# The first modulation rows as full-width products of the repeated silu(c), read in place by the first norm

## The chip, the cores and the metric

The kernel runs on one core of a Trainium2 chip. Its time is the device time of one execution in microseconds. The core has TensorE (PE, with its weight loads shown apart as PEld), VectorE (DVE), ScalarE (ACT), GpSimd (POOL) and the sync engine (SP), whose queue issues nearly all DMAs. PE writes to PSUM; the other engines read PSUM or SBUF.

## The reference

The kernel computes one transformer block with adaptive layer norm: attention without a softmax, then a mixture of eight experts. Two sequences of 1024 tokens, width 512, all float32. What matters here is how the first norm is modulated:

```python
mod = (_silu(L0_c) @ L0_wmod).reshape(L0_c.shape[0], 6, 1, -1)   # c: (2, 512), wmod: (512, 3072)
sa, ca, ga, sb, cb, gb = (mod[:, i] for i in range(6))
h = _layernorm(x, axis=-1) * (1 + ca) + sa
x = x + ga * attention(h)      # attention starts with a second layernorm, then K, V = Xn @ W_in + b_in
h = _layernorm(x, axis=-1) * (1 + cb) + sb
x = x + gb * moe(h)
```

Each of the six rows is one row of 512 values for each sequence. The first norm needs ca and sa of the first sequence on every one of the 128 partitions, since a partition holds a token.

## The kernel before

The 2048 tokens are 16 tiles of 128; tiles 0 to 7 are the first sequence, 8 to 15 the second, and four tiles share one x buffer and one buffer xnT of normed, transposed activations. For each tile t the kernel does: **norm1_in** (mean and variance of x: two DVE instructions, a square root on ACT, a reciprocal on DVE), **norm1_mid** (h = (x - mean) * (1 + ca)), **norm1_out** (h = h * rs + sa, then the second norm: statistics of h, sd, rs, off, and hn on ACT), **turn1** (four transposes of hn on PE into PSUM, four evictions by ACT into xnT), **kv_half** for K and for V (four products of 128x512 each, accumulated, evicted by DVE with the bias b_kv) and **kv_back** (squares, products and an accumulation on ACT, DVE and POOL). This loop over the tiles of the first sequence is the kernel's first stage; later come the projection, the second norm, the routing, the expert blocks and the shared expert.

Ahead of the loop stands the **opening**. PE first runs turn_over, products whose result nobody reads. The rows come from line 232, mod_parts: silu(c), padded to 32 columns in sc_pad, is the stationary operand, and the four 128-row pieces of the weights wm_ca (or wm_sa) are multiplied in four column strips of the array, each strip giving a partial sum for its piece k. ACT copies these partial sums to SBUF (parts). A second product, line 284, spread_product, has as its stationary operand one column of pick, repeated 128 times: it adds up the four partial sums of a sequence and puts the sum on all partitions at once. ACT copies that to SBUF, adding 1 for ca (spread_copy). The second sequence's rows are spread in the same place and copied a little later, though no tile before 8 reads them.

Buffers named by a home are shared: home 1 holds wm_sa first and xnT_0 afterwards, home 0 holds wm_ca and later wm_gb.

What orders the work: each engine runs its instructions in a fixed order. That order is made when the kernel is built, from the order in the program and a model of when inputs are ready, so it can differ from the program's. `tc.issue_after(ins)` puts the instructions in its block that run on ins's engine behind ins. DMAs go to SP's queue in the order of the load lines 152 to 204: c, wm_ca, the first x tile, wm_sa, cols, the other three x tiles of the group, the two halves of w_kv, b_kv, the rope table cs, and then the rest.

Of the kernel before, what the change touches and what calls it, by code (L numbers as in the profile page):

```python
# [18 lines left out]
P = 128  # L19
# [5 lines left out]
def kernel(  # L25
# [129 lines left out]
    def load_mod(m, home):  # L155
        t = act_tile(home, f"wmod{m}")
        nc.sync.dma_start(t, wm[:, :, m * D : (m + 1) * D])
        return t
# [3 lines left out]
    def load_x(g):  # L162
        t = xpool.tile([P, 4, D], FP, tag="x", name=f"x{g}")
        xs[g] = t
        for j0, j1 in ((0, 1), (1, 4)) if g == 0 else ((0, 4),):
            nc.sync.dma_start(t[:, j0:j1], xf[g][:, j0:j1])
            yield
# [40 lines left out]
    nc.vector.memset(ones_row, 1.0)  # L208
# [8 lines left out]
    nc.scalar.activation(sig_c, csb, AF.Sigmoid)  # L217
# [12 lines left out]
    copied = []  # L230

    def mod_parts(m, w, t):
        ps = mm_ps(f"mod_{m}")
        for k in range(KC):
            nc.tensor.matmul(
                ps[k * CT : (k + 1) * CT, :],
                sc_pad[:, k, :],
                w[:, k, :],
                start=True,
                stop=True,  # L240
                tile_position=(0, k * CT),
            )
        copied.append(nc.scalar.copy(t, ps))
# [35 lines left out]
    def own_parts(m, w):  # L279
        t = kvp.tile([P, D + 2 * R2], FP, tag="pr", name=f"parts_{m}")[:, 0:D]  # L280
        mod_parts(m, w, t)
        return t

    def spread_product(t, b, tag):
        ps = mm_ps(f"{tag}_{b}")
        nc.tensor.matmul(
            ps, pick[:, b : b + 1].to_broadcast([P, P]), t, start=True, stop=True
        )
# [7 lines left out]
    def spread_now(t, b, plus, tag):  # L296
        return spread_copy(spread_product(t, b, tag), b, plus, tag)
# [18 lines left out]
    aggregated = {}  # L316
# [9 lines left out]
    def normalize(dst, src, name):  # L326
        mv = small.tile([P, 2], FP, tag="mv", name=f"mv_{name}")
        rs = small.tile([P, 1], FP, tag="rs", name=f"rs_{name}")
        moments(mv, rs, src, name)
        off = small.tile([P, 1], FP, tag="off", name=f"off_{name}")  # L330
        nc.vector.tensor_scalar(off, mv[:, 0:1], -1.0, rs, ALU.mult, ALU.mult)
        nc.scalar.activation(dst, src, AF.Identity, bias=off, scale=rs)
# [15 lines left out]
    hn_of, turned1 = {}, {}  # L348
# [17 lines left out]
    def norm1_out(t):  # L366
        h, b = h_of.pop(t), t // NJ
        nc.vector.scalar_tensor_tensor(h, h, rs1[:, t : t + 1], sa[b], ALU.mult, ALU.add)
        hn_of[t] = ln.tile([P, D], FP, tag="hn", name=f"hn_{t}")
        normalize(hn_of[t], h, f"b{t}")  # L370
# [30 lines left out]
    fronts = {}  # L401
    waiting = []

    def kv_half(t, i):
# [4 lines left out]
        for k in range(KC):  # L409
            nc.tensor.matmul(  # L410
# [8 lines left out]
        )  # L419
        if i == 0 and waiting:  # L420

            with tc.issue_after(ins.ins):
                waiting.pop()()
# [636 lines left out]
    def second_rows():  # L1060


        return (
            spread_product(parts_ca, 1, "ca1"),
            spread_product(parts_sa, 1, "sa"),
        )

# [8 lines left out]
    def other_sums():  # L1076
# [8 lines left out]
        0: [],  # L1085
# [20 lines left out]
    norm1_out(0)  # L1106
    norm1_mid(1)
    turn1(0)
    with tc.issue_after(turned1[0].ins):
        ca1[1] = spread_copy(rows_1[0], 1, ones_t[:, 0:1], "ca1")  # L1110
        sa[1] = spread_copy(rows_1[1], 1, zero_t, "sa")
    norm1_out(1)
    acc = start_acc(0)
    for t in range(NJ):
        if t == 0:
            norm1_mid(2)
            norm1_out(2)

            nc.vector.scalar_tensor_tensor(
                cs[:, :, 0, :], cs[:, :, 1, :], -2.0, cs[:, :, 0, :], ALU.mult, ALU.mult  # L1120
            )
            nc.vector.scalar_tensor_tensor(
                cs[:, :, 1, :], cs[:, :, 1, :], -2.0, cs[:, :, 1, :], ALU.mult, ALU.mult
            )
            nc.vector.tensor_scalar(cs[:, :, 1, :], cs[:, :, 1, :], 1.0, None, ALU.add)
# [3 lines left out]
        turn1(t + 1)  # L1129
        for step in side[t]:  # L1130
            step()
        kv_half(t, 1)
# [575 lines left out]
```

## Time and profile before

| | us |
|---|---|
| median of 3 runs | 769.61 (768.76 to 770.23) |
| the profiled execution | 772.12 |
| its span, first to last instruction | 770.3 |
| PE busy | 751.9 |
| first stage opens: first kv product of tile 0 starts | 18.94 |

A line of a timeline reads: start in us, length in us (of a merged group: first start to last end), engine, line of the kernel, operation, output<-inputs, shape, count, and in brackets the idle time of that engine just before it with what ended it. A line of the waits or groups gives idle time by what released it. The granted clock of PE over the whole run was 0.994.

### The profile page before, as it was taken

Reading aid. Unit: us, or ns where it says so; the run is one execution under the profiler, and the core shown is the slowest. Engines: PE = TensorE matmul, PEld = TensorE weight load, DVE = VectorE, ACT = ScalarE, POOL = GpSimd, SP = SyncE. Lnnn points to the kernel's source line nnn. Section 1 sums busy time; section 2 is a strip of 40 time slices with the busy share of each in tenths; the row PEclk is TensorE's granted clock in tenths of the full one; section 3 lists DMA queues with packets and bytes.
Section 4 is the critical chain, followed back from the end, with each engine's and each line's share of the span. In section 5 each row is a group of like instructions: output and inputs, shape, how many; then the busy total and the mean of one; then the engine's idle time right before and its main releaser. Section 6 shows DMA issues by size and latency. Waiting matters only on the chain. (4 is left out here: it accounts for less than half of the span.)

```text
span 770.3 us, 8477 instructions
## 1 busy us (share of the span) xinstructions
PE 751.9 (98%) x2527; PEld 415.8 (54%) x2527; DVE 428.7 (56%) x979; ACT 232.5 (30%) x495; POOL 214.9 (28%) x241
## 2 busy tenths in 40 slices
PE   7999999999999999999999999999999998999997
PEld 2444444444444444684565656656566554888542
DVE  3888956898736888982222123222221121499964
ACT  4664523557643153110122122221221212122310
POOL 1234524863632687562100000000000000234530
PEclk9999999999999999999999999999999999999999
DMA  8950001212335711367999999999999884624551
GB/s 322 383 170 16 14 0 69 109 57 67 137 96 195 269 68 42 123 260 252 337 352 347 348 344 334 343 339 325 330 338 331 292 287 161 193 83 136 166 163 55
DMA packets 96369, 158.91 MB, mean 206 GB/s; under 512 B 8089, under 2 KB 51097, under 8 KB 96321
## 3 DMA queue, kind: packets, MB, share of 16 engines
q1 hardware_dynamic: 89984, 138.41, 53.6%
q0 software_dynamic: 5760, 18.88, 7.4%
q10 hardware_dynamic: 576, 1.05, 0.4%
q8 instruction: 22, 0.36, 0.2%
q14 instruction: 27, 0.21, 0.1%
HBM read 128.15 MB, written 30.16 MB: 206 GB/s over the span
## 5 line engine op out<-in xcount | busy, mean ns | idle before, releaser
L1360 POOL DMA_INDIRECT y<-ybuf,yrows x32 | 37.0, 1156 | 336.0 <-SPq L1586 288.4
L410 PE MATMUL kv<-w_kv,xnT 128*128 128x512 f32 x256 | 115.2, 596 | 0.5 <-ACT xnT L393 0.5
L1486 PE MATMUL by<-wd_r,gtT 128*128 128x512 f32 (+1 forms) x210 | 96.1, 593 | 0.8 <-DVEq L1578 0.8
L1458 PE MATMUL bg<-wg_r,hbT 128*128 128x352 f32 x280 | 88.9, 460 | 0.9 <-ACT y L1490 0.9
L1458 PE MATMUL bu<-wu_r,hbT 128*128 128x352 f32 x280 | 88.5, 459 | 0.0
L410 PEld LDWEIGHTS kv<-w_kv,xnT 128*128 128x128 f32 x256 | 46.9, 190 | 57.2 <-issue 48.1
L1458 PEld LDWEIGHTS bu<-wu_r,hbT 128*128 128x128 f32 x280 | 53.2, 190 | 29.6
L1473 DVE COPY gtT<-gtr 128x256 f32<-128x256 f32 x35 | 14.9, 425 | 97.0 <-PE gtr L1470 97.0
L1458 PEld LDWEIGHTS bg<-wg_r,hbT 128*128 128x128 f32 x280 | 50.4, 190 | 23.5 <-ACT y L1490 1.3
L571 PE MATMUL o<-wp,xnT 128*128 128x512 f32 x128 | 57.3, 593 | 0.0
L1337 DVE TENSOR_TENSOR sg_b<-sg_b,bg 128x352 f32<-128x352 f32 x35 | 18.3, 521 | 68.8 <-ACT sg_b L1336 68.8
L1486 PEld LDWEIGHTS by<-wd_r,gtT 128*128 128x128 f32 (+1 forms) x210 | 37.2, 191 | 34.5 <-issue 33.5
L1450 ACT COPY hbT<-tr_b 128x512 f32<-128x512 f32 x36 | 21.1, 586 | 101.1 <-PE tr_b L337 101.1
L1338 DVE TENSOR_TENSOR gt<-sg_b,bu 128x352 f32<-128x352 f32 x35 | 18.3, 521 | 47.2 <-PE bu L1458 47.2
L1490 ACT COPY y<-by 128x512 f32<-128x512 f32 x35 | 20.5, 586 | 70.7 <-PE by L1486 48.9
L571 PEld LDWEIGHTS o<-wp,xnT 128*128 128x128 f32 x128 | 23.8, 190 | 28.6 <-issue 27.0
L1336 ACT ACTIVATE sg_b<-bg 128x352 f32<-128x352 f32 x35 | 16.2, 464 | 76.1 <-PE bg L1458 76.1
L440 POOL TENSOR_TENSOR cross<-kv 128x128 f32<-128x128 f32 x16 | 12.6, 790 | 75.4 <-DVE kv L417 45.2
L530 PE MATMUL wp<-aw,wqT 128*128 128x512 f32 x64 | 30.0, 625 | 0.7 <-DVE aw L511 0.7
L433 ACT ACTIVATE sq<-kv 128x512 f32<-128x512 f32 x32 | 20.2, 630 | 27.2 <-DVE kv L417 25.6
L610 POOL TENSOR_TENSOR hr<-hr,cb 128x512 f32<-128x512 f32 x16 | 22.3, 1393 | 21.3 <-issue 7.2
L393 ACT ACTIVATE xnT<-tr_a,colsb 128x128 f32<-128x128 f32 x64 | 24.4, 455 | 11.0 <-PE tr_a L337 10.9
(319 smaller groups left out, 1264.7 us busy)
## 6 DMA issues: line engine op xcount, KB each, us to landing
wg_r<-in_w_gate_dram SPq DMA_DIRECT2D x35, 704.0 KB
wu_r<-in_w_up_dram SPq DMA_DIRECT2D x35, 704.0 KB
wd_r<-in_w_down_dram SPq DMA_DIRECT2D x35, 512.0 KB
hb<-hbuf SPq DMA_DIRECT2D x36, 256.0 KB
ybuf<-y SPq DMA_DIRECT2D x31, 256.0 KB
wd_r<-in_w_down_dram SPq DMA_DIRECT2D x35, 192.0 KB
wmod<-in_wmod_dram SPq DMA_DIRECT2D x6, 1024.0 KB
x<-in_x_dram SPq DMA_DIRECT2D x3, 1024.0 KB
```

Of the source, the lines that this page charges most:

```text
L393: turned1[t] = nc.scalar.activation(xnT[g][:, f, j * P : (j + 1) * P], ps[:, f * P : (f + 1) * P], AF.Identity, bias=colsb[:, 1, f : f + 1 ...
L410: nc.tensor.matmul(ps, xnT[g][:, k, j * P : (j + 1) * P], w_kv[:, i, k, :], start=(k == 0), stop=(k == KC - 1),)
L433: nc.scalar.activation(sq, kv[:, i, :], AF.Square, accum_out=ss[:, i : i + 1])
L530: nc.tensor.matmul(ps, wqT[:, k, f * P : (f + 1) * P], aw[:, k, :], start=(k == 0), stop=(k == KC - 1),)
L571: nc.tensor.matmul(ps, xnT[g][:, k, j * P : (j + 1) * P], wp[:, k, :], start=(k == 0), stop=(k == KC - 1),)
L610: nc.gpsimd.tensor_mul(h, h, cb1[b])
L1337: nc.vector.tensor_mul(sg[:m, :n], sg[:m, :n], pg[:m, :n])
L1360: nc.gpsimd.indirect_dma_start(out=y, out_offset=None, in_=ybuf, in_offset=bass.IndirectOffsetOnAxis(ap=yrows[:, t, s : s + 1], axis=0), b ...
L1450: nc.scalar.copy(hbT.rearrange("p k q -> p (k q)"), ps)
L1458: nc.tensor.matmul(ps[:, :H], hbT[:, k, :], wt[:, k, :], start=(k == 0), stop=(k == KC - 1))
L1486: nc.tensor.matmul(ps, gtT[:m, c, :], w[2][:m, c, :], start=(c == 0), stop=(c == NH - 1))
L1490: nc.scalar.copy(y, ps)
```

## The change

The rows are made in another way, and the opening is put in another order.

1. row_product takes the place of mod_parts and spread_product for ca and sa. One column of silu(c) is repeated 128 times as the stationary operand, and the four pieces of the weights are accumulated over the full array, so that the sum stands on all partitions at once. For ca a product of ones with a row of 1/128 is accumulated first, which adds the 1. The results stay in the PSUM pool sh (three buffers), and norm1_mid(0) and norm1_out(0) read them there; ACT copies them for the later tiles. The second sequence's row products come ahead of turn1(0), and their copies behind turn1(1).
2. wm_ca is loaded in two pieces, wm_sa in four, the first x tile ahead of both; the x tiles 2 and 3 behind the first half of w_kv; b_kv in two halves.
3. A square root of a constant behind the sigmoid loads ACT's table for it early.
4. norm1_in(1), norm1_out(1), norm1_in(2), norm1_mid(2) and norm1_out(2) get their places by issue_after. In the first pass of the loop both kv halves come ahead of turn1(1), and the three operations on cs come behind the second kv eviction.
5. turn_over has four products ahead of the rows instead of three, and none behind them.

mod_parts stays for the other four rows.

```diff
-    def load_mod(m, home):
+    def load_mod(m, home, pieces=1):
         t = act_tile(home, f"wmod{m}")
-        nc.sync.dma_start(t, wm[:, :, m * D : (m + 1) * D])
+        n = KC // pieces
+        for k in range(0, KC, n):
+            nc.sync.dma_start(t[:, k : k + n], wm[:, k : k + n, m * D : (m + 1) * D])
...
-        for j0, j1 in ((0, 1), (1, 4)) if g == 0 else ((0, 4),):
+        for j0, j1 in ((0, 1), (1, 2), (2, 4)) if g == 0 else ((0, 4),):
...
-    wm_ca = load_mod(1, 0)
     next(x_first)
-    wm_sa = load_mod(0, 1)
+    wm_ca = load_mod(1, 0, 2)
+    wm_sa = load_mod(0, 1, KC)
...
+    b_kv = epool.tile([P, 2 * D], FP, name="b_kv")
     for i in range(2):
-        nc.sync.dma_start(w_kv[:, i], wi[:, :, (i + 1) * D : (i + 2) * D])
-    b_kv = epool.tile([P, 2 * D], FP, name="b_kv")
-    nc.sync.dma_start(b_kv, b_in[D : 3 * D].partition_broadcast(P))
+        part = slice((i + 1) * D, (i + 2) * D)
+        nc.sync.dma_start(w_kv[:, i], wi[:, :, part])
+        nc.sync.dma_start(b_kv[:, i * D : (i + 1) * D], b_in[part].partition_broadcast(P))
+        if i == 0:
+            next(x_first)
...
-    nc.vector.memset(ones_row, 1.0)
+    nc.vector.memset(ones_row, 1.0 / P)
...
-    nc.scalar.activation(sig_c, csb, AF.Sigmoid)
+    sig = nc.scalar.activation(sig_c, csb, AF.Sigmoid)
+    with tc.issue_after(sig.ins):
+        nc.scalar.activation(
+            small.tile([P, 1], FP, tag="sd", name="sd_none"), eps_t, AF.Sqrt
+        )
...
-    def own_parts(m, w):
...
-    def spread_product(t, b, tag):
-        ps = mm_ps(f"{tag}_{b}")
-        nc.tensor.matmul(
-            ps, pick[:, b : b + 1].to_broadcast([P, P]), t, start=True, stop=True
-        )
+    def row_product(b, w, plus, tag):
+        ps = sh_ps(f"{tag}_{b}")
+        if plus:
+            nc.tensor.matmul(ps, ones_t, ones_row, start=True, stop=False)
+        for k in range(KC):
+            nc.tensor.matmul(
+                ps,
+                sc_pad[:, k, b : b + 1].to_broadcast([P, P]),
+                w[:, k, :],
+                start=(k == 0 and not plus),
+                stop=(k == KC - 1),
+            )
         return ps
-    def spread_copy(ps, b, plus, tag):
+    def row_copy(ps, b, tag):
         row = late.tile([P, D], FP, tag=tag, bufs=B, name=f"{tag}_{b}")
-        nc.scalar.activation(row, ps, AF.Identity, bias=plus)
+        nc.scalar.copy(row, ps)
         return row
...
-    turn_over(3, ones_row)
-    parts_ca = own_parts(1, wm_ca)
-    with tc.issue_after(copied[0].ins), tc.issue_after(silu.ins):
+    turn_over(4, ones_row)
+    with tc.issue_after(silu.ins):
         norm1_in(0)
-    ca1[0] = spread_now(parts_ca, 0, ones_t[:, 0:1], "ca1")
-    norm1_in(1)
-    parts_sa = own_parts(0, wm_sa)
+
+    ca1[0] = row_product(0, wm_ca, True, "ca1")
     norm1_mid(0)
-    sa[0] = spread_now(parts_sa, 0, zero_t, "sa")
-    turn_over(2, parts_sa)
-    rows_1 = second_rows()
-    norm1_in(2)
+    ca1[0] = row_copy(ca1[0], 0, "ca1")
+    sa[0] = row_product(0, wm_sa, False, "sa")
     norm1_out(0)
-    norm1_mid(1)
+    sa[0] = row_copy(sa[0], 0, "sa")
+    rows_1 = [row_product(1, wm_ca, True, "ca1"), row_product(1, wm_sa, False, "sa")]
+    with tc.issue_after(aggregated["b0"].ins):
+        norm1_in(1)
+        norm1_mid(1)
     turn1(0)
-    with tc.issue_after(turned1[0].ins):
-        ca1[1] = spread_copy(rows_1[0], 1, ones_t[:, 0:1], "ca1")
-        sa[1] = spread_copy(rows_1[1], 1, zero_t, "sa")
-    norm1_out(1)
+    with tc.issue_after(turned1[0].ins), tc.issue_after(off_made["b0"].ins):
+        norm1_out(1)
+    with tc.issue_after(off_made["b1"].ins):
+        norm1_in(2)
     acc = start_acc(0)
     for t in range(NJ):
         if t == 0:
-            norm1_mid(2)
-            norm1_out(2)
...
+            with tc.issue_after(off_made["b1"].ins):
+                norm1_mid(2)
         else:
             norm1(t + 2)
         kv_half(t, 0)
-        turn1(t + 1)
-        for step in side[t]:
-            step()
-        kv_half(t, 1)
+        if t == 0:
+            kv_half(t, 1)
+            with tc.issue_after(kv_last[t].ins):
+                turn1(t + 1)
+            with tc.issue_after(turned1[t + 1].ins):
+                norm1_out(2)
+                ca1[1] = row_copy(rows_1[0], 1, "ca1")
+                sa[1] = row_copy(rows_1[1], 1, "sa")
+            with tc.issue_after(evicted[t].ins):
...
+        else:
+            turn1(t + 1)
+            for step in side[t]:
+                step()
+            kv_half(t, 1)
         kv_back(t, acc)
```

More of the change, by code (lines that the diff above doesn't have):

```diff
@@ L228 @@
     parts = {}
-    copied = []
     def mod_parts(m, w, t):
@@ L242, in mod_parts @@
             )
-        copied.append(nc.scalar.copy(t, ps))
+        nc.scalar.copy(t, ps)
     def mod_sums(*ws):
@@ L277, in spread @@
         return t
-    def own_parts(m, w):
-        t = kvp.tile([P, D + 2 * R2], FP, tag="pr", name=f"parts_{m}")[:, 0:D]
-        mod_parts(m, w, t)
-        return t
-    def spread_product(t, b, tag):
-        ps = mm_ps(f"{tag}_{b}")
-        nc.tensor.matmul(
-            ps, pick[:, b : b + 1].to_broadcast([P, P]), t, start=True, stop=True
-        )
+    def row_product(b, w, plus, tag):
[10 more added lines that the diff above has]
+            )
         return ps
-    def spread_copy(ps, b, plus, tag):
+    def row_copy(ps, b, tag):
         row = late.tile([P, D], FP, tag=tag, bufs=B, name=f"{tag}_{b}")
-        nc.scalar.activation(row, ps, AF.Identity, bias=plus)
+        nc.scalar.copy(row, ps)
         return row
-    def spread_now(t, b, plus, tag):
-        return spread_copy(spread_product(t, b, tag), b, plus, tag)
     modT = late.tile([P, 2, KC, B], FP, name="modT")
@@ L314 @@
     rs1 = const.tile([P, NT], FP, name="rs1")
-    aggregated = {}
+    aggregated, off_made = {}, {}
     def moments(mv, rs, src, name):
@@ L330, in normalize @@
         off = small.tile([P, 1], FP, tag="off", name=f"off_{name}")
-        nc.vector.tensor_scalar(off, mv[:, 0:1], -1.0, rs, ALU.mult, ALU.mult)
-        nc.scalar.activation(dst, src, AF.Identity, bias=off, scale=rs)
+        off_made[name] = nc.vector.tensor_scalar(
+            off, mv[:, 0:1], -1.0, rs, ALU.mult, ALU.mult
+        )
+        return nc.scalar.activation(dst, src, AF.Identity, bias=off, scale=rs)
     def transposes(src, name):
@@ L346 @@
         raise ValueError("the homes are laid out for two sequences of two groups")
-    hn_of, turned1 = {}, {}
+    hn_of, hn_made, turned1 = {}, {}, {}
     h_of = {}
@@ L369, in norm1_out @@
         hn_of[t] = ln.tile([P, D], FP, tag="hn", name=f"hn_{t}")
-        normalize(hn_of[t], h, f"b{t}")
+        hn_made[t] = normalize(hn_of[t], h, f"b{t}")
     def norm1(t):
@@ L401 @@
     fronts = {}
+    kv_last, evicted = {}, {}
     waiting = []
@@ L409, in kv_half @@
         for k in range(KC):
-            nc.tensor.matmul(
+            kv_last[t] = nc.tensor.matmul(
                 ps,
@@ L419, in kv_half @@
         )
+        evicted[t] = ins
         if i == 0 and waiting:
@@ L1058, in start_acc @@
         return kvp.tile([P, D + 2 * R2], FP, tag="acc", bufs=1, name=f"acc_{b}")
[L1060 to L1066, printed above, removed]
     def own(m, w):
@@ L1084 @@
     side = {
-        0: [],
         1: [lambda: own(2, wm_ga)],
@@ L1115 @@
         if t == 0:
-            norm1_mid(2)
-            norm1_out(2)
[L1119 to L1125, printed above, removed]
+            with tc.issue_after(off_made["b1"].ins):
+                norm1_mid(2)
         else:
@@ L1128 @@
         kv_half(t, 0)
-        turn1(t + 1)
-        for step in side[t]:
-            step()
-        kv_half(t, 1)
+        if t == 0:
[7 more added lines that the diff above has]
+            with tc.issue_after(evicted[t].ins):
+                nc.vector.scalar_tensor_tensor(
+                    cs[:, :, 0, :], cs[:, :, 1, :], -2.0, cs[:, :, 0, :], ALU.mult, ALU.mult
+                )
+                nc.vector.scalar_tensor_tensor(
+                    cs[:, :, 1, :], cs[:, :, 1, :], -2.0, cs[:, :, 1, :], ALU.mult, ALU.mult
+                )
+                nc.vector.tensor_scalar(
+                    cs[:, :, 1, :], cs[:, :, 1, :], 1.0, None, ALU.add
+                )
+        else:
[3 more added lines that the diff above has]
+            kv_half(t, 1)
         kv_back(t, acc)
```

## The prediction

> **What bounds the kernel now.** I read the busy table first, then the list of what TensorE (PE) waited for, then the timelines of PE, its weight loads (PEld), ACT, DVE and the DMA issues over the first 60 us. The busy table:
>
> ```profile
> PE 751.9 (98%) x2527; PEld 415.8 (54%) x2527; DVE 428.7 (56%) x979; ACT 232.5 (30%) x495; POOL 214.9 (28%) x241
> ```
>
> PE is busy throughout; all of its listed waits in the whole run come to some 14 us, the largest 2.0. So once the first tile has opened, a microsecond put in front of PE comes out at the end, unless a later PE wait takes it up. The change touches the opening only, and there PE looks like this (start, duration, name, count):
>
> ```profile
> 1.63 5.46 PE L213 MATMUL turn_over<-ones_row,ones_t 128*128 128x512 f32 x6 [1.63 <-DVE ones_row L208]
> 7.02 1.23 PE L235 MATMUL mod<-wmod,sc_pad 128*32 128x512 f32 x8
> 8.97 1.12 PE L286 MATMUL ca<-parts,pick 128*128 128x512 f32 x2 [0.72 <-ACT parts L243]
> 10.29 1.06 PE L235 MATMUL mod<-wmod,sc_pad 128*32 128x512 f32 x8 [0.20 <-DMA wmod<-in_wmod_dram]
> 12.06 1.12 PE L286 MATMUL sa<-parts,pick 128*128 128x512 f32 x2 [0.71 <-ACT parts L243]
> 13.02 1.88 PE L213 MATMUL turn_over<-parts,ones_t 128*128 128x512 f32 x4
> 14.74 1.02 PE L286 MATMUL ca<-parts,pick 128*128 128x512 f32 x2
> 15.60 1.02 PE L286 MATMUL sa<-parts,pick 128*128 128x512 f32 x2
> 17.73 0.66 PE L337 MATMUL tr_a<-ident,hn 128*128 128x128 f32 x4 [1.11 <-ACT hn L332]
> 18.94 4.56 PE L410 MATMUL kv<-w_kv,xnT 128*128 128x512 f32 x10 [0.55 <-ACT xnT L393]
> 23.33 0.60 PE L337 MATMUL tr_a<-ident,hn 128*128 128x128 f32 x4
> 23.77 6.17 PE L410 MATMUL kv<-w_kv,xnT 128*128 128x512 f32 x14
> 29.95 0.66 PE L337 MATMUL tr_a<-ident,hn 128*128 128x128 f32 x4
> ```
>
> The reader should see two things. Each f32 product of 512 columns is **two** instructions (the three products of turn_over(3) show as x6). And the four-strip products of line 235 put eight instructions into 1.06 us, because they stand beside each other in four column strips. The first tile's transposes at 17.73 waited not for PE but for hn, the last step of the first norm. The weight loads give the pace of one instruction, cold and warm:
>
> ```profile
> 5.18 0.34 PEld L213 LDWEIGHTS turn_over<-ones_row,ones_t 128*128 128x128 f32 x1 [0.52 <-issue]
> 14.74 0.19 PEld L286 LDWEIGHTS ca<-parts,pick 128*128 128x128 f32 x1 [0.24 <-issue]
> ```
>
> 0.34 + 0.52 = 0.86 us per instruction at the start, 0.19 + 0.24 = 0.43 later. Line 286 is already a product whose stationary operand is one column repeated 128 times, so 0.43 is the row for the new products too; the 14 kv instructions at 23.77 (6.17 us) keep the same pace.
>
> **What is removed.** Two mod groups (16 instructions), four spread products (8), two turn_over products of parts (4), and from ACT two copies of parts and the +1/+0 evictions in the first tile's chain. Between 7.02 and 17.73 PE worked about 7 of 10.7 us; the rest was hops to ACT and back (0.72, 0.71) and the wait for hn (1.11).
>
> **What is added.** One more turn_over product (2 instructions) and four row products: ca has ones plus four k (10 instructions), sa four k (8), for two sequences: 36 instructions x 0.43 = 15.4 us of PE, where 16 + 8 + 4 went before. All four row products come ahead of turn1(0) in the program. More than order holds them there: xnT_0 has home 1, which is wm_sa's buffer, so the first eviction of turn1(0) must wait until the last sa product, that of the second sequence, has read wm_sa.
>
> **The opening, step by step.** Six cold instructions run from 1.63 to about 6.89 (the sixth starts near 6.03). The mod group at 7.02 took 1.23 where the warm one took 1.06; 0.17 lost at half pace means the clock rose about 0.34 after 7.02, at 7.36. Then: seventh and eighth turn_over, one half cold, end at 7.98; ones, 0.86, 8.84; four k of ca, 3.43, 12.27; sa, 3.43, 15.70; ca of the second sequence, 4.29, 19.99; its sa, 3.43, **23.4**. The transposes start there, against 17.73: **+5.7 us**.
>
> Is hn late instead? DVE and ACT give the old chain:
>
> ```profile
> 14.34 0.72 DVE L368 SCALAR_TENSOR_TENSOR h<-h,rs,sa 128x512 f32<-128x512 f32 x1
> 16.87 0.81 ACT L332 ACTIVATE hn<-h,off_b,rs_b 128x512 f32<-128x512 f32 x1 [0.48 <-DVE off_b L331]
> ```
>
> From h to the end of hn is 3.34 us. With sa read in place at 15.8, hn ends at about 19.2, 1.5 later than now, and has 4.2 us to spare under the second sequence's products. So the hops, copies and the early table load that the change saves are worth nothing at this point: PE is late next. A PSUM operand on DVE is near the kv eviction (0.68) and under the same cover; gone, it would cost tenths.
>
> **A rule against the row.** The Trainium skill ("TensorE: Matmul & The Clock Gate", section "Back-to-back issue gap") says that in a stream of weight load and matmul pairs 512 columns come to about 131 ns per matmul, against 216 isolated. Applied as a ratio to 0.43 that is an estimate of 0.26 us per instruction: the 36 would take 9.4 us, transposes could start at 7.98 + 9.4 = 17.4, and hn would be what is awaited. The row shows 0.43 in unbroken streams of the very shape, so I take 15.4. The same page ("The HAM clock gate") has the clock rise after some 3.4 us of activity: from 1.63 that is 5.04, which would end the turn_overs near 6.8 and the products at 22.2, a loss of 4.5 instead of 5.7. The cold pace at 5.18 and the long group at 7.02 speak for the later time in this execution; the 4.5 stays as a low end.
>
> **Transfers.** The queue's issues now:
>
> ```profile
> 1.28 0.42 SPq L157 DMA_DIRECT2D wmod<-in_wmod_dram  x1
> 1.76 0.50 SPq L166 DMA_DIRECT2D x<-in_x_dram  x1
> 2.30 0.44 SPq L157 DMA_DIRECT2D wmod<-in_wmod_dram  x1
> ```
>
> The pieces add six issues, at some 0.44 each 2.6 us of SP's time up to the rope tables, but the same bytes, and the stretch's 350 to 400 GB/s says the engines, not the issues, set the pace. x0 plus wm_ca are 1.31 MB as before (x0, last of them, was used at 7.16), wm_sa lands by about 10.3 and is needed from 12.3, w_kv from 24: 2 us and more of cover. Without it PE would stand for the lag itself.
>
> **After the opening.** turn1(1) now follows all 16 kv instructions of tile 0, so kv of tile 1 waits for an eviction: the first such place cost 0.55. I take 0.2 (between 0, if own(2) is drawn into the hole as the transposes of line 497 are mixed with kv at 40, and 0.7). norm1_out(1) and norm1_out(2) have ACT behind the evictions of tile 0 and tile 1: sd, off, hn take some 2 us there and have a kv half (3.4) or more of time. The old wait before 29.95 (the load of 28.92 ends its 0.43 at 29.35: 0.6) should go; kept, it costs 0.6. The three cs operations (1.22 + 1.21 + 0.67) move behind tile 0's last eviction; POOL's first pr waits for them, and DVE adds acc later still, so I put them at 0 with 0.3 as upper end. The second rows' copies (0.7 each) queue on ACT ahead of kv_back's squares; PE reads none of it: 0. Sum: 5.7 + 0.2 - 0.6 = **+5.3**.
>
> The sum is made on a span of 770.3 in an execution of 772.1, so 775.6 of span; the median of the runs, 769.61, lies 2.5 under that execution and takes the same step: **774.9 us**.
>
> **Rivals.**
> - *Pulled apart:* the order on the engines lets sa of the second sequence go before its ca, and transposes and kv start with ca's 4.3 us still to do, of which the waits of 18 to 45 (0.55, 0.6, 0.48, 0.35, together 2.0) take up some. For it: PE's order does differ from the program's at 40. Against: 26 instructions stand before the transposes anyway (19.1). About +1.4 + 4.3 - 2.0 = +3.7: 773.3.
> - *Other side, a faster product:* if an instruction in this stream costs under (17.73 - 7.98) / 36 = 0.27 us, PE is not late and only hn counts. At 0.26, ca ends at 7.98 + 10 x 0.26 = 10.6 and sa at 12.7, hn at 12.8 + 3.34 = 16.1, the 36 at 17.4: -0.3, and -0.6 for the stall at 29.95: 768.7, or 767.5 if the clock also rose by the rule's 5.04. Only the rule above speaks for it.
> - *Absorbed:* some later wait hides it, no change. The PE waits after 60 us are for DVE and ACT results that shift along, so little speaks for this: 769.6.
> - *Worse:* the clock rises later, a gap before tile 1 and one before tile 2, +7.5 or more: 777.1.
>
> **How the numbers follow.** Forecast (+4.0 to +7.4) 0.78, pulled apart 0.08, worse 0.06, absorbed 0.02, faster product 0.06 (0.04 with the clock's help, 0.02 without). A change under 0.2% (1.5 us) can't be told from none here: faster 0.04, same 0.02 + 0.02 = 0.04, slower 0.92. The range goes from +2.6 (clock rule 4.5, less 0.6, 0.48, 0.35, less some of ca) to +7.4 (products 0.6 later, gap 0.7, old stall kept, cs 0.3): 772.2 to 777.0.
>
> **What would show it.** In the changed kernel: row products at 0.43 per instruction without holes from about 9 to 23; hn of tile 0 done near 19 and PE's transposes not waiting for it; transposes at 23 to 24; the stall before tile 2 gone. I am wrong if the products pack closer, if the transposes start before 21, or if PE's waits in 25 to 60 differ from now by more than 1.5 us.

## The result, and the profile after

| | before | changed |
|---|---|---|
| median of 6 runs each, us | 769.39 (768.76 to 771.88) | 776.89 (775.85 to 779.03) |
| the profiled execution | 772.12 | 777.01 |
| its span | 770.3 | 775.1 |
| PE busy | 751.9 | 759.8 |
| transposes of tile 0 start | 17.73 | 22.28 |

The changed kernel is slower: ratio 1.009, 95% interval 1.0074 to 1.0106, or 5.7 to 8.2 us. A second set of runs of the same file (the experiment "changed again" below) gave 776.64 beside 770.47: +6.2.

The busy table of the changed kernel:

```profile
PE 759.8 (98%) x2537; PEld 420.8 (54%) x2537; DVE 426.8 (55%) x979; ACT 231.1 (30%) x494; POOL 217.3 (28%) x241
```

PE has 10 instructions more, net, and 7.9 us more of work. Its share is 98% in both: what is put in front of it is not absorbed. PE's timeline over the opening and the first tiles of the changed kernel:

```profile
1.63 5.36 PE L218 MATMUL turn_over<-ones_row,ones_t 128*128 128x512 f32 x8 [1.63 <-DVE ones_row L213]
6.83 1.02 PE L292 MATMUL ca<-ones_row,ones_t 128*128 128x512 f32 x2
7.69 3.60 PE L294 MATMUL ca<-wmod,sc_pad 128*128 128x512 f32 x8
11.12 3.60 PE L294 MATMUL sa<-wmod,sc_pad 128*128 128x512 f32 x8
14.55 1.02 PE L292 MATMUL ca<-ones_row,ones_t 128*128 128x512 f32 x2
15.41 3.60 PE L294 MATMUL ca<-wmod,sc_pad 128*128 128x512 f32 x8
18.85 3.60 PE L294 MATMUL sa<-wmod,sc_pad 128*128 128x512 f32 x8
22.28 0.60 PE L348 MATMUL tr_a<-ident,hn 128*128 128x128 f32 x4
23.43 7.13 PE L422 MATMUL kv<-w_kv,xnT 128*128 128x512 f32 x16 [0.55 <-ACT xnT L404]
30.40 0.60 PE L348 MATMUL tr_a<-ident,hn 128*128 128x128 f32 x4
31.55 3.70 PE L422 MATMUL kv<-w_kv,xnT 128*128 128x512 f32 x8 [0.55 <-ACT xnT L404]
35.18 1.05 PE L243 MATMUL mod<-wmod,sc_pad 128*32 128x512 f32 x2
36.16 0.66 PE L348 MATMUL tr_a<-ident,hn 128*128 128x128 f32 x4
36.74 1.06 PE L243 MATMUL mod<-wmod,sc_pad 128*32 128x512 f32 x6
```

The order is the program's: two row products, two more, then tile 0. From 7.69 to 22.28 no line has a bracket, so PE waited for nothing. Each group starts 3.43 after the one before it where that had eight instructions, 0.86 where it had two: 0.43 per instruction. At 22.28 hn of tile 0 has long been ready; on ACT's timeline it ended at 18.35:

```profile
17.55 0.80 ACT L343 ACTIVATE hn<-h,off_b,rs_b 128x512 f32<-128x512 f32 x1
```

To say where the time went, take the start of each tile's transposes of hn in both timelines and subtract (tile 0 from 17.73, then 23.33, 29.95, 38.50 and 49.97 in the kernel before). The changed kernel is later by 4.55, 7.07, 6.21, 6.20 and 5.48 us at tiles 0 to 4; its repeat by 5.36, 7.88, 7.01, 7.01 and 6.29. In the step to tile 1, 2.57 is no loss: six kv instructions of tile 0 that stood behind turn1(1) now stand ahead of it. The opening thus lost 4.55 and 5.36, the stretch from tile 0 to tile 4 lost **0.93 in both**, and little happens after that (the first profiled span ends 4.8 later, the repeat's 6.0).

Executions of one kernel differ by how often their granted clock is lowered. In the profiles of this case the clock falls to half for 3.4 us at a time; up to the last 10 us of the span, the profiles with a mean clock of 0.999 have no such stretch, those with 0.997 have one, those with 0.994 or 0.995 have two. The times follow: the kernel before takes about 769.1 at a mean of 0.999, 770.3 at 0.997, 772 at 0.994. Small differences below are therefore also given between the means of runs of equal mean clock. At 0.997 the changed kernel took 776.5 (4 runs of the second set) beside 770.2 (8 runs): +6.3, where the sum forecast +5.3. This measure has a limit: where a kernel itself brings about such a stretch or does away with one, equal clocks leave that part of its effect out.

### The profile page after: what moved, and what is told of

Same layout as the page of the kernel before. It is cut to its first block, busy times and chain, and to the rows that moved or that the text cites. A ratio compares the mean times of both kernels' runs of the same rounds, so it can differ in the third digit from the quotient of the medians.

```text
span 775.1 us, 8501 instructions
## 1 busy us (share of the span) xinstructions
PE 759.8 (98%) x2537; PEld 420.8 (54%) x2537; DVE 426.8 (55%) x979; ACT 231.1 (30%) x494; POOL 217.3 (28%) x241
## 5 line engine op out<-in xcount | busy, mean ns | idle before, releaser
L429 DVE TENSOR_TENSOR kv<-kv,b_kv 128x512 f32<-128x512 f32 x32 | 21.7, 679 | 12.4 <-PE kv L422 12.4
```

Of the source, the lines that this page charges most:

```text
L429: ins = nc.vector.tensor_add(fronts[t][:, i, :], ps, b_kv[:, i * D : (i + 1) * D])
```

## The experiments

The theory: PE is the queue that sets the end; the full-width products lengthen it by what the four-strip form did not cost, and the new order adds gaps. The rivals: the order alone does it (the second sequence's products ahead of tile 0), the loads do it, or later waits make it larger or smaller.

**1. The second sequence's products left out.** This kernel leaves out the row products of the second sequence and takes the first's rows in their place.

```diff
-    ca1[0] = row_product(0, wm_ca, True, "ca1")
+    ca1[0] = ps_ca = row_product(0, wm_ca, True, "ca1")
...
-    sa[0] = row_product(0, wm_sa, False, "sa")
+    sa[0] = ps_sa = row_product(0, wm_sa, False, "sa")
...
-    rows_1 = [row_product(1, wm_ca, True, "ca1"), row_product(1, wm_sa, False, "sa")]
+    rows_1 = [ps_ca, ps_sa]
```

> The changed kernel without the two row products of the second sequence (18 of the 36 instructions, 7.7 us of PE); the second sequence takes the first's rows, so its part of the output is computed from those. Theory W (PE's added work ahead of the first tile is the loss): transposes of tile 0 no longer wait behind products but for hn, which ended at 18.35 in the changed kernel, so they start near 18.4 instead of 22, and the time falls by 3.5 to 4 us, to about 773. Rival C (the loads in pieces, the norm order and the loop order carry the loss): the time stays within 1.5 us of the changed kernel's 776.9.

Measured: 774.7 (773.8 to 776.4), ratio 1.0057 (1.0036 to 1.0078). Its PE timeline:

```profile
12.42 3.60 PE L294 MATMUL sa<-wmod,sc_pad 128*128 128x512 f32 x8
19.69 0.66 PE L348 MATMUL tr_a<-ident,hn 128*128 128x128 f32 x4 [3.68 <-ACT hn L343]
20.90 8.83 PE L422 MATMUL kv<-w_kv,xnT 128*128 128x512 f32 x16 [0.55 <-ACT xnT L404]
```

With 7.7 us of products gone, only 2.6 come off the opening (tile 0 is 1.96 later than in the kernel before): now hn is late, and PE stands 3.68 for it. Another 1.3 is the execution's and not the kernel's: ca's first product starts at 8.13 here and at 6.83 in the changed kernel, because PE reached its full pace later. Counted from there, tile 0 comes 3.9 sooner, as expected. Then the sixteen kv instructions take 8.83 where they take 7.13 in the changed kernel. So a second effect hides part of the gain, and the next run takes it away.

**2. The same, with the hole filled.** As in 1, rows of the second sequence taken from the first, with three turn_over products behind the last row product (the edit is shown against experiment 1).

```diff
-            nc.tensor.matmul(
+            kv_last["row"] = nc.tensor.matmul(
...
     rows_1 = [ps_ca, ps_sa]
+    with tc.issue_after(kv_last["row"].ins):
+        turn_over(3, ones_row)
```

> The first experiment's kernel (second sequence's products left out, its rows taken from the first's) with three turn_over products in the hole of 3.7 us behind sa. They compute nothing. In the first experiment the pace of PE fell to 0.86 per instruction behind that hole for some 4 us. If this cost what its trace shows, the kernel is 1.5 to 2 us faster than that one, about 773; if the hole did no harm in most executions, the same, 774.7.

Measured: 774.57 (772.01 to 775.01), ratio 1.0035 (1.0022 to 1.0047). PE's timeline of this kernel:

```profile
14.92 2.74 PE L218 MATMUL turn_over<-ones_row,ones_t 128*128 128x512 f32 x6
18.76 0.65 PE L348 MATMUL tr_a<-ident,hn 128*128 128x128 f32 x4 [1.10 <-ACT hn L343]
19.97 7.13 PE L422 MATMUL kv<-w_kv,xnT 128*128 128x512 f32 x16 [0.55 <-ACT xnT L404]
```

And one window of 2 us of each kernel, the one with the hole first, then the filled one (window, its length, busy time and count of PE, PEld, DVE, ACT and POOL, granted clock, DMA share, GB/s):

```profile
21.00:23.00 2.00, 2.00 (x3) 0.87 (x4) 1.48 (x6) 1.19 (x4) 0.00 (x0) 0.57 1.06 371
```

```profile
21.00:23.00 2.00, 2.00 (x6) 0.88 (x5) 1.37 (x7) 1.14 (x3) 0.00 (x0) 1.00 1.06 379
```

The granted clock is 0.57 against 1.00, and PE runs 3 instructions in the time of 6. Filling the hole keeps the clock and brings kv back to 7.13. Of the gain in the total I can say less: the medians differ by 0.1, the ratios by some 1.7 us, and the expected 773 was met only by the runs at 0.997 (772.6, 6 of 17). Experiment 1's runs at 0.995 took 774.4, and its profile has two lowered stretches, one of them the opening's; one stretch less is worth the 1.7 that the kv instructions lost. The other runs here have lowered stretches later on. The profile shows the mechanism; its worth in the median stays open. Against the changed kernel at 0.997 (776.5), the second sequence's products cost 3.9 here.

**3. The second sequence's products later.** Is it only their place ahead of tile 0? They go behind turn1(1), and wm_sa gets a buffer of its own so that xnT_0 need not wait for it.

```diff
-    wm_sa = load_mod(0, 1, KC)
+    wm_sa = load_mod(0, 5, KC)
...
-    rows_1 = [row_product(1, wm_ca, True, "ca1"), row_product(1, wm_sa, False, "sa")]
...
+            with tc.issue_after(kv_last[t].ins):
+                rows_1 = [
+                    row_product(1, wm_ca, True, "ca1"),
+                    row_product(1, wm_sa, False, "sa"),
+                ]
```

> The changed kernel with the same two row products of the second sequence moved behind turn1(1); wm_sa gets home 5 so that xnT_0 needn't wait for them. No work is left out. Theory W (amount of work): the transposes of tile 0 start near 18.4, but PE then stands idle from about 14.5 to 18.4 and does the 7.7 us later, of which only the 0.55 gap before tile 1 is hidden: 3 us slower than the changed kernel, about 780. Rival O (order: what hurts is that they stand ahead of the first tile): 3.5 to 4 us faster than the changed kernel, about 773.

Measured: 778.65 (777.72 to 780.1), ratio 1.0106 (1.0085 to 1.0126): 1.8 above the changed kernel. PE's timeline:

```profile
19.22 0.66 PE L348 MATMUL tr_a<-ident,hn 128*128 128x128 f32 x4 [3.68 <-ACT hn L343]
20.43 8.78 PE L422 MATMUL kv<-w_kv,xnT 128*128 128x512 f32 x16 [0.55 <-ACT xnT L404]
```

Tile 0 starts 3 us sooner than in the changed kernel, but the hole and the slow kv are back, and most of the 7.7 us of the 18 instructions is paid behind them: tile 2's transposes come 10.69 later than before, against 6.21. From tile 0 to tile 2 the lag grows by 9.20, in experiment 1, without these products, by 3.41: 5.8 of the 7.7 are paid, and the rest covers waits that experiment 1 has there. The order rival, which expected 773, falls, even if the 1.7 us of slow kv are taken off; the 780 of the theory was too much. In the changed kernel these products at least lie over the wait for hn.

**4. The new order without full-width products.** The four-strip products and the spread are kept, everything else of the change stays, the reading in PSUM too.

```diff
-    turn_over(4, ones_row)
+    turn_over(3, ones_row)
+    parts_ca = own_parts(1, wm_ca)
...
-        for k in range(KC):
-            nc.tensor.matmul(
-                ps,
-                sc_pad[:, k, b : b + 1].to_broadcast([P, P]),
-                w[:, k, :],
-                start=(k == 0 and not plus),
-                stop=(k == KC - 1),
-            )
+        nc.tensor.matmul(
+            ps, pick[:, b : b + 1].to_broadcast([P, P]), t, start=not plus, stop=True
+        )
...
```

> Everything of the change but its products: the rows come again from four column strips and a spread product (with two idle products of parts behind), and are read in place by the first norm. Theory W: the opening is set by data and by the hops again; sa's strips at 10.3, copy to 12.0, spread to 12.9, h at 13.0, hn at 16.4, transposes at 16.5 against 17.73 before; with the gap ahead of tile 1 (some 0.9 in the changed kernel) about 769, within 1 us of the kernel before. Rival C: most of the 7.5 us remain, 773 or more.

Measured: 771.48 (769.44 to 773.43), ratio 1.0012 (0.9999 to 1.0025). PE's timeline, tile 0:

```profile
17.86 0.60 PE L346 MATMUL tr_a<-ident,hn 128*128 128x128 f32 x4
```

Tile 0's transposes start 0.13 later than before. They were expected at 16.5; hn ends at 17.36, and PE's queue is last here too, since this kernel keeps the ones products of ca, 0.86 each, and its strips wait for the second piece of wm_ca (until 8.4). At a clock of 0.997 this is 771.3 against 776.5: **the full-width products are worth 5.2 of the 6.3 us**. Of what is left, the trace shows 0.13 at tile 0 and 1.46 at tile 2: it lies in the order behind the opening.

**5. turn1(1) back between the kv halves.** The changed kernel with the old order of the first pass.

```diff
         kv_half(t, 0)
+        turn1(t + 1)
         if t == 0:
-            kv_half(t, 1)
-            with tc.issue_after(kv_last[t].ins):
-                turn1(t + 1)
...
```

> The changed kernel with turn1(1) between the two kv halves of tile 0, as before. Theory W with the loop order as a small term: the 0.55 wait ahead of kv of tile 1 goes and the transposes of tile 2 don't wait for hn, 0.5 to 1 us faster than the changed kernel, about 776. If the loop order was needed (hn of tile 1 late), 0 to 1 us slower, about 777.5.

Measured: 773.33 (772.0 to 775.51), ratio 1.0039 (1.0025 to 1.0052): 3.6 under the changed kernel in medians, 2.2 at equal clock (774.2), where 0.5 to 1 was expected. PE's timeline:

```profile
27.18 0.60 PE L348 MATMUL tr_a<-ident,hn 128*128 128x128 f32 x4
27.61 7.03 PE L422 MATMUL kv<-w_kv,xnT 128*128 128x512 f32 x16
34.48 0.60 PE L348 MATMUL tr_a<-ident,hn 128*128 128x128 f32 x4
35.01 1.06 PE L243 MATMUL mod<-wmod,sc_pad 128*32 128x512 f32 x8
```

Here tile 1's kv needs no eviction when it comes up, since the second half of tile 0 stands in between: kv follows the transposes after 0.43, not 1.15, and the eight mod instructions stay together. The opening is the changed kernel's (+4.76 at tile 0); from there to tile 4 this kernel gains 1.54 on the kernel before instead of losing 0.93. Of the 1.54, 1.26 come between tiles 3 and 4, where the kernel before waits at the wqT transposes (0.48 and 0.35) and this one, being later, does not.

**6. Both put back.** Experiment 4 with the order of 5.

In the expectation, the third and fourth kernel are experiments 4 and 5.

> The third kernel (strips in the new order) with turn1(1) between the halves as before. If the loop order costs 2 to 3 us whatever the rows are made of, as the fourth kernel showed with full-width products: 2 to 2.5 us faster than the third kernel's 771.5, about 769.2, that is at or some 1 us below the kernel before. If the fourth kernel's gain was tied to the late opening, no more than 1 us of it shows here, 770.5 or more.

Measured: 771.0 (769.01 to 773.36), ratio 0.9998 (0.9986 to 1.0009), which is no difference from before and 1.8 above what was expected. The order that is worth 2.2 behind full-width products is worth 0.2 at equal clock here, 0.5 in medians, 1.1 by the two ratios. The trace shows where the rest goes: at tile 2's transposes this kernel is 1.40 ahead of experiment 4, at tile 4's only 0.32, and between them PE waits for an eviction at the wqT transposes:

```profile
42.87 1.13 PE L508 MATMUL wqT<-ident,w_q 128*128 128x128 f32 x8 [1.37 <-ACT xnT L402]
```

An earlier PE meets a wait there that a later one does not.

**7. Only the loads.** The kernel before with the pieces and the order of the loads, nothing else.

```diff
-    wm_ca = load_mod(1, 0)
     next(x_first)
-    wm_sa = load_mod(0, 1)
+    wm_ca = load_mod(1, 0, 2)
+    wm_sa = load_mod(0, 1, KC)
...
```

> The kernel before with the loads of the change alone (pieces, x0 ahead, x2 and x3 and b_kv moved). As predicted the bytes ahead of wm_ca's and wm_sa's last piece hardly change: within 0.5 us of the kernel before. Rival C (the loads carry part of the loss): 1 us slower or more.

Measured: 774.6 (772.12 to 778.25), ratio 1.005 (1.0031 to 1.0068): +3.9 from loads of the same bytes in medians and by the ratio, +2.0 at a clock of 0.997, the highest of its runs (772.4). The weight loads' timeline, DVE's, then PE's, of this kernel:

```profile
8.11 0.14 PEld L240 LDWEIGHTS mod<-wmod,sc_pad 128*32 128x32 f32 x4 [0.95 <-DMA wmod<-in_wmod_dram]
```

```profile
15.18 0.75 DVE L373 SCALAR_TENSOR_TENSOR h<-h,rs,sa 128x512 f32<-128x512 f32 x1 [2.09 <-ACT sa L298]
16.39 0.69 DVE L325 BATCH_NORM_STATS2 st_a<-x 128x6 f32<-128x512 f32 x1 [0.46 <-DMA x<-in_x_dram]
17.00 0.68 DVE L325 BATCH_NORM_STATS2 st_b<-h 128x6 f32<-128x512 f32 x1
```

```profile
19.63 0.66 PE L342 MATMUL tr_a<-ident,hn 128*128 128x128 f32 x4 [1.84 <-ACT hn L337]
20.83 6.13 PE L415 MATMUL kv<-w_kv,xnT 128*128 128x512 f32 x10 [0.55 <-ACT xnT L398]
```

Tile 0's transposes come 1.90 later than before, in two parts. The second piece of wm_ca lands late and the strips wait for it, and on ACT the copy of sa's partial sums stands behind the square root for tile 1, whose x comes late: the second h of tile 0 (15.18) is 0.84 later. Then, on DVE, the statistics of tile 2's x stand ahead of tile 0's own (st_b). That x is used only at 16.39, so tile 0's hn is late by another 1.06 for data it does not need. PE's hole becomes 1.84, its clock falls once more (0.50 at 21 to 23), and ten kv instructions take 6.13 instead of 4.56. Ahead of tile 2 the order built into this kernel splits own(2) too, though hn has been ready since 32.93, and 0.9 more is lost. In the changed kernel the issue_after of norm1_in(1) and norm1_in(2) puts those statistics behind tile 0's, and PE waits for no DMA there. That the late x tiles are harmless only together with that move is read from these two traces; no run has the one without the other in the changed kernel.

**8. The reading in place, with the statistics moved.** The kernel before, with sa of tile 0 read in PSUM and the statistics of tiles 1 and 2 behind tile 0's.

```diff
-    norm1_in(1)
...
-    sa[0] = spread_now(parts_sa, 0, zero_t, "sa")
+    sa[0] = sa_ps = spread_product(parts_sa, 0, "sa")
...
-    norm1_in(2)
     norm1_out(0)
-    norm1_mid(1)
+    sa[0] = spread_copy(sa_ps, 0, zero_t, "sa")
+    with tc.issue_after(aggregated["b0"].ins):
+        norm1_in(1)
+        norm1_mid(1)
+        norm1_in(2)
```

> The kernel before with one part of the change alone: norm1_out(0) reads sa in PSUM, and the statistics of tiles 1 and 2 stand behind tile 0's norm on DVE. h then starts at about 13.0 instead of 14.34 and hn ends 1.3 earlier; PE's filler ends at 16.6. If the opening before was bound by this chain, as predicted: 0.8 to 1.2 us faster than the kernel before. If PE's filler or the norms of tiles 1 and 2 are late next: within 0.4 us of it.

Measured: **769.15** (768.15 to 771.61), ratio 0.9975 (0.9965 to 0.9986): the lowest median of all, 1.1 to 2.7 us under the kernel before. At a clock of 0.997, 769.4 against 770.4. PE's timeline, then DVE's:

```profile
17.06 0.66 PE L337 MATMUL tr_a<-ident,hn 128*128 128x128 f32 x4 [0.54 <-ACT hn L332]
```

```profile
13.13 0.75 DVE L368 SCALAR_TENSOR_TENSOR h<-h,rs,sa 128x512 f32<-128x512 f32 x1 [1.07 <-PE sa L286]
15.38 0.67 DVE L320 BATCH_NORM_STATS2 st_a<-x 128x6 f32<-128x512 f32 x1
15.97 0.20 DVE L331 TENSOR_SCALAR off_b<-mv_b,rs_b 128x1 f32<-128x1 f32 x1
```

h starts 1.21 sooner, but hn, expected 1.3 sooner, comes only 0.67 sooner, since moved statistics now stand on DVE ahead of off_b. The lead of 0.66 to 0.67 still stands at tile 3. The part of the change that shortens the chain to hn does pay, where PE waits for hn. The two edits were not tried apart. In the trace of before, the copy of sa ends at 13.97 and the statistics of tiles 1 and 2 hold DVE until h starts at 14.34, so in that order neither edit alone could have brought h to 13.13.

**9. The same, pushed further.** The statistics of tiles 1 and 2 behind off of tile 0, and one turn_over product less, since PE no longer has to wait so long. The edit is shown against experiment 8, which the expectation calls the sixth.

```diff
-    turn_over(2, parts_sa)
+    turn_over(1, parts_sa)
...
-    with tc.issue_after(aggregated["b0"].ins):
+    with tc.issue_after(off_made["b0"].ins):
...
```

> The sixth experiment's kernel (before, sa read in place) with the statistics of tiles 1 and 2 behind off instead of behind the second norm's statistics, and one turn_over product less behind the rows. Off stood at 15.97 there with 0.5 us of other statistics ahead of it; hn should end about 0.5 earlier, and tile 0's transposes start near 16.5. If the first norm's chain still sets the opening: 0.3 to 0.6 us faster than the sixth kernel's 769.2. If the norms of tiles 1 and 2 become late: the same or slower.

Measured: 769.47 (767.81 to 771.89), ratio 0.999 (0.998 to 1.0). Tile 0's transposes start at 16.38, 1.35 sooner than before, but the lead is down to 0.79 at tile 4, given back at the wqT transposes, where PE waits 1.20 instead of 0.48. It is not better than experiment 8: at a clock of 0.997, 769.5 against 769.4.

**10. The changed kernel again,** unchanged.

> The changed kernel itself once more, beside the two others of this call, to size its loss with more executions. The nearest pairs at an equal mean clock (0.997) gave 776.4 against 770.3 before: theory W expects a difference of 5.5 to 7 us at equal clock, and a profile in which kv of tile 0 starts 4.5 to 6 us later than before, depending on when the clock rose.

Measured: 776.64 (776.32 to 778.43), ratio 1.0077 (1.0059 to 1.0096). Its kv of tile 0 starts at 24.24, 5.30 later than before.

**11. Four more products.** The changed kernel with eight more PE instructions (3.43 us) of no use ahead of turn1(0). If PE is the queue they cost 3.43, if there is slack, less.

```diff
-            nc.tensor.matmul(
+            kv_last["row"] = nc.tensor.matmul(
...
+    with tc.issue_after(kv_last["row"].ins):
+        turn_over(4, ones_row)
...
     turn1(0)
```

> The changed kernel with four turn_over products more (8 instructions, 3.43 us, computing nothing) between the second sequence's rows and turn1(0). Theory W, PE's queue ahead of tile 0 is the bound: the whole 3.43 us comes out at the end, 3 to 3.8 slower than the changed kernel. If hn or a load sets the opening, less than 2.

Measured: 781.51 (778.92 to 782.42), ratio 1.0136 (1.0115 to 1.0157). That is +4.9 on the run of the changed kernel beside it in medians, +3.95 at equal clock (780.45 against 776.5). PE's timeline:

```profile
21.97 3.60 PE L218 MATMUL turn_over<-ones_row,ones_t 128*128 128x512 f32 x8
25.40 0.60 PE L348 MATMUL tr_a<-ident,hn 128*128 128x128 f32 x4
```

The eight instructions take 3.43 from start to start, and up to tile 4 nothing later takes it up: all five starts of transposes are 3.12 or 3.13 later than in the first trace of the changed kernel, in which PE reached its full pace 0.31 later. The 0.5 on top at equal clock isn't explained; it rests on three runs of 778.9 to 782.4.

**12. The cs operations behind off of tile 2.** own(2) is the group of eight mod instructions, the row ga in four strips, that follows tile 2's transposes in the kernel before. Why is it split in the changed kernel (35.18 and 36.74)? DVE's timeline of the changed kernel, then ACT's:

```profile
33.27 0.15 DVE L333 RECIPROCAL rs_b<-sd_b 128x1 f32<-128x1 f32 x1
33.34 1.46 DVE L1138 SCALAR_TENSOR_TENSOR cs<-cs 128x1024 f32<-128x1024 f32 x1
34.72 0.20 DVE L340 TENSOR_SCALAR off_b<-mv_b,rs_b 128x1 f32<-128x1 f32 x1
```

```profile
34.96 0.81 ACT L343 ACTIVATE hn<-h,off_b,rs_b 128x512 f32<-128x512 f32 x1 [0.47 <-DVE off_b L340]
```

The change moved the cs operations behind tile 0's second eviction, and there one of them, 1.46 long, stands between rs_b and off_b of tile 2 (before, it was the last of the three, 0.67 long, at 28.13). hn ends at 35.77; PE was free at 34.98, and the order built into the kernel has one strip of own(2) in that place. This kernel moves the three operations a little further, and nothing else by hand:

```diff
-            with tc.issue_after(evicted[t].ins):
+            with tc.issue_after(off_made["b2"].ins):
                 nc.vector.scalar_tensor_tensor(
                     cs[:, :, 0, :], cs[:, :, 1, :], -2.0, cs[:, :, 0, :], ALU.mult, ALU.mult
                 )
```

> The changed kernel with the three cs operations behind off of tile 2 on DVE instead of behind tile 0's second kv eviction; nothing else is moved by hand. Theory: the cs operations (the second of them 1.46 us, at 33.34) stand on DVE between rs_b and off_b of tile 2, so hn of tile 2 ended at 35.77 while PE was free at 34.98, and the order built into the kernel put one strip of own(2) into that hole, paying 0.98 plus 0.2. Without them off_b comes at about 33.5, hn ends near 34.6, the four strips of own(2) stay in one group behind the transposes, and the transposes of tile 2 start some 1.1 us sooner counted from tile 0 (lag grows by about 0.5 from tile 0 to tile 2 instead of 1.66). If that lead lives to the end: about 775.3 at a mean clock of 0.997 (changed kernel 776.5). Rival: the lead is met by the waits at the wqT transposes (0.72 there), and the end moves by 0.4 or less: about 776.1. Second rival: hn of tile 2 is late for another reason (its statistics behind tile 1's transposes), then the transposes wait 0.6 to 0.8 and nothing is gained.

Measured: 774.14 (773.34 to 775.44), ratio 1.0043 (1.0027 to 1.006), with 771.92 before beside it. PE's timeline of this kernel:

```profile
32.19 3.70 PE L422 MATMUL kv<-w_kv,xnT 128*128 128x512 f32 x8 [0.55 <-ACT xnT L404]
35.73 0.60 PE L348 MATMUL tr_a<-ident,hn 128*128 128x128 f32 x4
36.26 1.06 PE L243 MATMUL mod<-wmod,sc_pad 128*32 128x512 f32 x8
```

off_b now comes at 33.60, hn of tile 2 ends at 35.04, the group of eight is whole again and the transposes wait for nothing. From tile 0 to tile 2 the lag grows by 0.59 (5.19 to 5.78) where it grew by 1.66, and at tile 4 it is 4.41: -0.78 from tile 0 on, where the changed kernel has +0.93. So no later wait took the lead up, and neither rival holds. In the total, seven of its runs have a clock of 0.999 and take 774.1, 5.0 more than the kernel before at that clock (769.1); the one run at 0.997 takes 775.4, against 776.5 of the changed kernel. At equal clock the move is worth 1.1 to 1.3 us, in the opening's trace 1.7. In medians it is 2.5: none of the changed kernel's twelve runs has a clock of 0.999, and seven of eight have it here. Whether the move itself spares the later lowered stretches was not tested.

## Why the prediction was right, and where it was not

The direction and the mechanism hold: PE's queue, lengthened by 36 instructions at 0.43, sets the opening. The range holds by 0.1: the median of 776.89 lies 2.0 above the forecast of 774.9 and just under the upper end of 777.0, whose parts add up to +7.3 and not +7.4. That it holds so narrowly is in part the clock's doing: the difference of the medians is +7.5, at equal clock it is +6.3. And in the sum two misses offset each other: the opening lost 0.3 to 1.2 less than forecast, the stretch behind it 1.3 more. That the two together, 5.5 and 6.3 in the two traces, lie near the forecast of 5.3 is luck. By steps:

- **36 instructions at 0.43, PE late next.** Shown. In both traces of the changed kernel they run unbroken at 0.43, hn ends 3.9 us before PE is free (the prediction had 4.2), and experiments 4 and 11 show that PE's queue is what costs: take the products out and 5.2 us go; add eight and all of their time is paid. The saved copies and hops are worth nothing here and something only where PE waits for hn (experiment 8), as the prediction had it; the early table load (1.28 us, on ACT at 2.69 instead of 8.93) lies under the same cover. One reading was off without harm: between 7.02 and 17.73 PE had worked 8.0 us and not about 7.
- **The rule of 131 ns against the row.** The row decides. "Back-to-back issue gap" of the Trainium skill's "TensorE: Matmul & The Clock Gate", scaled, would have had four k in 2.1 us, an estimate; they took 3.43, all four times. The rival "a faster product" falls.
- **The opening, +5.7.** It measured 4.55 and 5.36. The term that varies is the time at which PE reaches its full pace, taken here as the clock's rise. The profile's clock does not show it: in the first trace it stands at 1.00 from 2 to 4 us, where PE runs 3 instructions, and from 5.5 to 7.5, where it runs 6. The weight loads show where the pace goes from 0.34 + 0.52 to 0.19 + 0.24: at 5.11 in the first trace, at 6.78 in the repeat, at 4.80 in experiment 11:

```profile
4.32 0.34 PEld L218 LDWEIGHTS turn_over<-ones_row,ones_t 128*128 128x128 f32 x1 [0.52 <-issue]
5.11 0.19 PEld L218 LDWEIGHTS turn_over<-ones_row,ones_t 128*128 128x128 f32 x1 [0.45 <-issue]
```

```profile
6.03 0.34 PEld L218 LDWEIGHTS turn_over<-ones_row,ones_t 128*128 128x128 f32 x1 [0.52 <-issue]
6.78 0.19 PEld L218 LDWEIGHTS turn_over<-ones_row,ones_t 128*128 128x128 f32 x1 [0.42 <-issue]
```

```profile
4.80 0.19 PEld L218 LDWEIGHTS turn_over<-ones_row,ones_t 128*128 128x128 f32 x1 [0.24 <-issue]
```

  I had carried 7.36 over from the one profile of before. The same page's "The HAM clock gate" says that the window of some 3.4 us runs free of the kernel's start; counted from 1.63, one full busy window would end anywhere from 5.04 to an estimated 8.5 (two windows). In the traces of the changed kernel and of the experiments that open with the same products the first short load comes from 4.80 to 7.70 (experiment 1): a spread of that kind, but the earliest lies before the page's 5.04, and the measurement decides. So neither 4.5 nor 5.7 was the number of the change: the rise differs between executions of one kernel, and comparing the two traces puts 0.8 us of it into the difference.
- **After the opening, -0.4 (a gap of 0.2, a stall of 0.6 that goes).** This is the mis-sized term: it measured **+0.93** in both traces, 1.3 off, with three parts. *First*, the gap ahead of tile 1's kv was put at 0.2; it measured 0.71 (transposes at 30.40 to kv at 31.55 is 1.15, before it was 0.44). own(2) was not drawn into the hole, and 0.55 had been the row to take. *Second*, the cs operations, put at 0 with 0.3 as upper end: I asked who waits for their result (POOL's pr) and not what stands behind them on DVE. off_b of tile 2 did, so its hn came late, and the order built into the kernel has own(2) split around the transposes. One strip alone takes 0.98, nearly as long as the 1.06 of eight instructions in four strips side by side, so the split pays that price twice, and 0.2 of waiting ahead of it. Experiment 12 takes this alone away, and the stretch to tile 4 then measures -0.78. That this is near the -0.4 of the forecast is luck: it is +0.59 up to tile 2 and -1.37 from there to tile 4, where PE, being later, meets none of the waits at the wqT transposes. The kernel before had own(2) in one piece:

```profile
30.54 1.06 PE L235 MATMUL mod<-wmod,sc_pad 128*32 128x512 f32 x8
31.53 7.13 PE L410 MATMUL kv<-w_kv,xnT 128*128 128x512 f32 x16
```

  *Third*, the stall before 29.95 that was to go was never 0.6. I took the last kv's weight load and added 0.43:

```profile
28.92 0.19 PEld L410 LDWEIGHTS kv<-w_kv,xnT 128*128 128x128 f32 x1 [0.24 <-issue]
```

  A weight load can start while the product before its own is still on: kv's group at 23.77 is 14 x 0.43 = 6.0 long and so ends near 29.8. The stall was about 0.17, and so was the gain. The three make 0.71 + 0.98 + 0.2 - 0.17 = 1.72; a gap ahead of tile 0's kv that is 0.06 shorter (1.15, before 1.21) makes it the 1.66 measured from tile 0 to tile 2. At the wqT transposes PE, now later, then finds 0.72 less to wait for, the part that the prediction had kept for its low end. Experiment 5 takes the gap and the split away, and +0.93 becomes -1.54.
- **Transfers at nothing.** Right for the change: no PE wait before 60 us names a DMA. But the reason given, the same bytes and 2 us of cover, was not enough. Experiment 7 shows that the new load order by itself costs 3.9 us in the kernel before, or 2.0 at equal clock, through a late piece of wm_ca and through statistics that wait for x ahead of tile 0's. In the changed kernel those statistics stand elsewhere, and the prediction did not name them.
- **The rivals.** "Pulled apart" did not occur. "Absorbed" is refuted by experiment 11. "Worse" named 777.1, from a later clock and gaps ahead of tiles 1 and 2; the first median came out close to it, but only the gaps were there, the clock rose sooner, and at equal clock the loss is 6.3.

## What to carry to other kernels

Where PE is busy 98% of the time, count its instructions before its neighbours' waits: a product that spares ACT two hops and PE nothing is paid in full, even at the opening, once it is longer than the wait it replaces. Take an idle engine's cover from the trace as a budget (here the opening's four waits of PE, 0.72, 0.20, 0.71 and 1.11 us) and keep the part of a change that fits into it; here the gain was the reading in place together with the moved statistics. Of an operation that is moved "where nobody needs it", read the queue that it is moved into: three operations on DVE, of which nobody wants the result for a while, held up the one small instruction that tile 2's transposes needed.

## What the runs showed of the hardware

- PE reached its full pace between 4.8 (experiment 11) and 7.7 us (experiment 1) in different executions, while it always started at 1.63; the profile's clock shows 1.00 on both sides of the step.
- After a PE hole of 3.68 us the granted clock fell for the kv products that followed, and 2.74 us of idle products in that hole kept it at 1.00. This fits the stretch of about 3.4 us that the Trainium skill gives ("TensorE: Matmul & The Clock Gate", "HAM oscillation"). Experiment 7 shows that the longest single hole is not the measure: it fell there after holes of 1.84 and 0.55 us with only four transposes between. If the transposes are counted as part of the hole, PE was without products for 3.0 us there and for 4.9 in experiments 1 and 3; where the clock held, it was 2.3 (before, and experiment 2) or less. The 3.0 lie under the page's 3.4. That this is what counts has not been tested.
- The same lowering occurs near 100 and near 660 us, each time for 3.4 us: the profile of before has a clock of 0.50 from 100 to 103, that of experiment 5 has 1.00 in the same stretch of its work. Such stretches come and go from execution to execution, and a run's mean clock goes with its time: 769.1 at 0.999 and 772 at 0.994 for one and the same kernel.
- Four strips of 512 columns side by side (eight instructions) took 1.06 us, one alone (two instructions) 0.98, and four such pieces of the weights over the full array 3.43.
